# First layer of a two-layer kernel: norm, transpose and copy of a token tile issued in front of the key products of the tile ahead of it

## The chip, the cores and the metric

The kernel runs on one core of a Trainium2 chip. The metric is device time in microseconds (us). A core has a matrix engine (TensorE, PE in the profile; its weight loads are PEld), a vector engine (VectorE, DVE), an engine for activation functions and copies (ScalarE, ACT), a general engine (GpSimd, POOL) and a queue that issues most transfers (SyncE, SP). The engines run side by side and wait for each other by semaphores; each works through its own list of instructions in the order of that list. SBUF is the memory on the core from which they work, PSUM the one that TensorE writes its results to.

## The reference

One sequence of 2048 tokens of width 512, float32, passes two layers. Each layer norms the tokens and adds an attention and a feed-forward part to them. Only the head of the first layer matters here:

```python
xn = _layernorm(x, axis=-1)
x = x + _L0_attn_ref(xn, ...) + _L0_ffn_ref(xn, ...)

# in _L0_attn_ref: linear attention, 16 heads of 32
k = _heads(hidden_states @ k_w.T + k_b, b, s)
v = _heads(hidden_states @ v_w.T + v_b, b, s)
kp = jax.nn.elu(k) + 1.0
kv = jnp.einsum('bhsd,bhse->bhde', kp, v)
z = jnp.einsum('bhsd,bhd->bhs', qp, kp.sum(axis=2))[..., None]
# in _L0_ffn_ref: 8 of 16 experts for each token
probas = jax.nn.sigmoid(x2 @ Wg.T)
_, idx = jax.lax.top_k(probas + biases, K)
```

The second layer has causal attention over a window of 1024 tokens, and a block that runs attention and an MLP on an eighth of the tokens. The change doesn't touch it.

## The kernel before, in words

**The whole.** `two_layer_kernel` has one stage after another: the head stage of the first layer (keys, the sum over keys, the experts' ranks), then queries, experts and output projection in four blocks of 512 tokens, then both parts of the second layer. The change lies in the head stage, which in the profile reaches from the start to some 144 us of 1706.2.

**The loop.** The stage goes over 16 tiles of 128 tokens (`NT = 16`, `for t in range(NT)`). One round for tile t writes down, in this order:

- at t = 0, 4 and 8: the loads of the four tiles t+4 to t+7 (`load_x`, line 70, SP queue), and their mean and variance (`stats`, lines 74, 75 on VectorE; the root at line 78 on ScalarE, its reciprocal at line 79). At t = 0 the weights of the later stages are put on the SP queue too.
- the norm: `xn = (x - mean) * rstd`, one VectorE instruction (line 276); GpSimd adds the output bias to the unnormed tile (line 280), and SP stores that sum in DRAM (`res_d`, line 70).
- `transpose4` (line 110): four 128x128 transposes of `xn` on TensorE into a PSUM tile `tr`, and one ScalarE copy (line 117) from there to `xnT`.
- the key products `pk` (line 288): four matmuls of 512 columns, from `xnT` and the key weights. In the profile each float32 matmul stands as two instructions, so a tile has 8.
- the key's feature map: VectorE adds the bias (line 290, `kk`) and cuts at zero (line 293, `ke`), ScalarE takes the exponential (line 294), VectorE joins both (line 295, `kk`), and GpSimd adds the result to a running sum (line 296, `ksum`).
- `gathered(t - 1)` (line 242): four matmuls of 512 columns, `gx += kk^T xn`, for the tile before. They read its `kk` and its `xn`.
- after t = 3, 7 and 11: `gates` for the block of four tiles (products `pgp`, line 204; a ScalarE copy `gp`, line 117; products `pg`, line 212; an exponential, line 215), then `ranked` (lines 222 to 235), 23 VectorE instructions that rank the 16 experts of each token. The last block's come after the loop.

**Buffers.** Tile `x` has 8 buffers, `xn` has 3, `kk` and `ke` have 2 each, and PSUM has 2 for `tr` (shared with `pg`) and 2 for `pk` (shared with `pgp`). A buffer is reused when its last reader is done: the fourth `xn` waits for the `gathered` of the first.

**What sets the order.** The kernel is written with a framework that builds each engine's list. It doesn't keep the source's order: an instruction that is ready by its own estimate of times may go ahead of an earlier one that isn't, and among those that are ready the one written first goes first. The trace shows both: the transposes of tiles 1 and 2 stand side by side on TensorE at 14.14 us, and one pair of `gx` instructions of the tile before stands between a tile's transposes and its `pk`. Once built, a list is fixed.

Of the kernel before, what the change touches and what calls it, by code (L numbers as in the profile page):

```python
# [12 lines left out]
F32 = mybir.dt.float32  # L13
BF16 = mybir.dt.bfloat16
AF = mybir.ActivationFunctionType
ALU = mybir.AluOpType
# [3 lines left out]
P = 128  # L20
T = 2048
NT = T // P
D = 512
# [15 lines left out]
def two_layer_kernel(ctx: ExitStack, tc: tile.TileContext, a: dict, out: bass.AP):  # L39
    nc = tc.nc  # L40
    V, S, G, PE = nc.vector, nc.scalar, nc.gpsimd, nc.tensor
# [4 lines left out]
    def const(shape, name, pool=cpool, dtype=F32):  # L46
        return pool.tile(shape, dtype, tag=name, name=name)
# [19 lines left out]
    res_d = tc.dram_tile([T, D], F32, name="res_d")  # L67

    def load(eng, dst, src):
        eng.dma_start(out=dst, in_=src)  # L70
# [35 lines left out]
    def transpose4(pool, src_of, dst, name, copy, tag="tr"):  # L106

        tp = pool.tile([P, NC, P], F32, tag=tag, name=name)
        for c in range(NC):
            PE.transpose(tp[:, c, :], src_of(c), ident)  # L110
        copy(dst, tp)
# [16 lines left out]
    with ExitStack() as l0:  # L128
# [3 lines left out]
        def weight(name, shape, src, pool=w0):  # L132
            t = const(shape, name, pool)
            load(nc.sync, t, src)
            return t

        xnT = [const([P, NC, TB], f"xnT{b}", xp) for b in range(NTB)]
# [6 lines left out]
        with ExitStack() as p1:  # L144
            w1 = p1.enter_context(tc.tile_pool(name="w1", bufs=1))
            wk1 = p1.enter_context(tc.tile_pool(name="wk1", bufs=2))
            ps_kv = p1.enter_context(tc.tile_pool(name="ps_kv", bufs=1, space=PSUM))
            ps1 = p1.enter_context(tc.tile_pool(name="ps1", bufs=2, space=PSUM))

            kc = "(c p) o -> p c o"  # L150
            x = {}

            def load_x(t):
                x[t] = wk1.tile([P, D], F32, tag="x", name=f"x_{t}", bufs=8)
                load(nc.sync, x[t], a["x"][t * P : (t + 1) * P, :])
# [15 lines left out]
            ob = weight("ob", [P, D], a["o_b"].partition_broadcast(P), w1)  # L171
# [17 lines left out]
            mv = const([P, NT, 2], "mv", w1)  # L189
            rstd = const([P, NT], "rstd", w1)  # L190
            def stats(lo, hi):
                for t in range(lo, hi):
                    layernorm_stats(wk1, mv[:, t, :], x[t], f"st_{t}")
                rsqrt_into(rstd[:, lo:hi], mv[:, lo:hi, 1], eps5)
# [4 lines left out]
            def gates(b):  # L199


                parts = ps1.tile([P, TB], F32, tag="mm", name=f"pgp_{b}")
                for c in range(NC):
                    PE.matmul(
                        parts[c * HD : (c + 1) * HD, :], WgT[:, c, :], xnT[b][:, c, :],
                        start=True, stop=True, skip_group_check=True,
                    )
                gp = wk1.tile([P, TB], F32, tag="gp", name=f"gp_{b}", bufs=1)
                scopy(gp, parts)
                pg = ps1.tile([P, 4, E], F32, tag="tr", name=f"pg_{b}")  # L210
                for i in range(4):
                    PE.matmul(
                        pg[:, i, :], gp[:, i * P : (i + 1) * P], fold, start=True, stop=True
                    )
                S.activation(prob[:, 4 * b : 4 * b + 4, :], pg, AF.Exp, scale=-1.0)

            def ranked(b):

                pr = prob[:, 4 * b : 4 * b + 4, :]
                V.tensor_scalar_add(pr, pr, 1.0)
                V.reciprocal(pr, pr)
                sc = wk1.tile([P, 4, E], F32, tag="sc", name=f"sc_{b}", bufs=1)
                V.tensor_tensor(sc, pr, rb.unsqueeze(1).to_broadcast([P, 4, E]), ALU.add)
                for i in range(4):
                    other = sc[:, i, :].unsqueeze(1).to_broadcast([P, E, E])
                    own = sc[:, i, :].unsqueeze(2).to_broadcast([P, E, E])
                    gt = wk1.tile([P, E, E], F32, tag="gt", name=f"gt_{b}_{i}")
                    eq = wk1.tile([P, E, E], F32, tag="eq", name=f"eq_{b}_{i}")  # L230
                    V.tensor_tensor(gt, other, own, ALU.is_gt)
                    V.tensor_tensor(eq, other, own, ALU.is_equal)
                    V.tensor_tensor(eq, eq, tie, ALU.mult)
                    V.tensor_tensor(gt, gt, eq, ALU.add)
                    V.tensor_reduce(rank[:, 4 * b + i, :], gt, AX.X, ALU.add)
# [4 lines left out]
            def gathered(t, kk, xn):  # L240
                for g in range(NC):
                    PE.matmul(  # L242
                        gx[g], kk[:, g * P : (g + 1) * P], xn, start=t == 0, stop=t == NT - 1
                    )

            before = None
            for t in range(NT):
                tok = slice(t * P, (t + 1) * P)
                xt = xnT[t // 4][:, :, t % 4 * P : (t % 4 + 1) * P]
                if t % 4 == 0 and t + 4 < NT:  # L250
                    for u in range(t + 4, t + 8):
                        load_x(u)
                    stats(t + 4, t + 8)
                if t == 0:
                    q_b = weight("q_b", [P, NC], a["q_b"])

                    q_wT = weight("q_wT", [P, NC, D], a["q_wT"].rearrange(kc, p=P))
                    WdT = weight("WdT", [P, NC, LAT], a["WdT"].rearrange(kc, p=P))
                    sw1T = weight("sw1T", [P, NC, HID], a["sw1T"].rearrange(kc, p=P))
                    swgT = weight("swgT", [P, NC, HID], a["swgT"].rearrange(kc, p=P))  # L260
                    rw1T = weight("rw1T", [P, E, HID], a["rw1T"])
                    rwgT = weight("rwgT", [P, E, HID], a["rwgT"])
                    rw2T = weight(
                        "rw2T", [P, 2, E, LAT], a["rw2T"].rearrange("(b p) e l -> p b e l", p=P)
                    )
                    o_wT = weight("o_wT", [P, NC, D], a["o_wT"].rearrange(kc, p=P))
                    sw2T = weight("sw2T", [P, 2, D], a["sw2T"].rearrange(kc, p=P))
                    WuT = weight("WuT", [P, D], a["WuT"])
                    wr = weight("wr", [P, D], a["w_router"].partition_broadcast(P))
                    for j in range(2):  # L270
                        load(
                            nc.sync, w_qk[:, :, j * D : (j + 1) * D],
                            a["w_qkv"][:, j * D : (j + 1) * D].rearrange(kc, p=P),
                        )
                xn = wk1.tile([P, D], F32, tag="xn", name=f"xn_{t}", bufs=3)
                V.tensor_scalar(
                    xn, x[t], mv[:, t, 0:1], rstd[:, t : t + 1], ALU.subtract, ALU.mult
                )

                G.tensor_tensor(x[t], x[t], ob, ALU.add)  # L280
                load(nc.sync, res_d[tok, :], x[t])
                transpose4(
                    ps1, lambda c: xn[:, c * P : (c + 1) * P], xt, f"tr_{t}", scopy
                )

                pk = ps1.tile([P, D], F32, tag="mm", name=f"pk_{t}")
                for c in range(NC):
                    PE.matmul(pk, xt[:, c, :], k_wT[:, c, :], start=c == 0, stop=c == NC - 1)  # L288
                kk = wk1.tile([P, D], F32, tag="kk", name=f"kk_{t}")
                V.tensor_tensor(kk, pk, kb, ALU.add)  # L290

                ke = wk1.tile([P, D], F32, tag="ke", name=f"ke_{t}")
                V.tensor_scalar_min(ke, kk, 0.0)
                S.activation(ke, ke, AF.Exp)
                V.scalar_tensor_tensor(kk, kk, 0.0, ke, ALU.max, ALU.add)
                G.tensor_tensor(ksum, ksum, kk, ALU.add)
                if before is not None:
                    gathered(*before)
                before = t, kk, xn
                if t % 4 == 3 and t < NT - 1:  # L300
                    gates(t // 4)
                    ranked(t // 4)
# [34 lines left out]
        with ExitStack() as p3:  # L337
# [127 lines left out]
            for b in range(NTB):  # L465
# [76 lines left out]
                for i in range(TB // P):  # L542
                    t = b * (TB // P) + i
                    xr.append(wk.tile([P, D], F32, tag="xr", name=f"xr_{t}", bufs=4))
                    load(nc.sync, xr[i], res_d[t * P : (t + 1) * P, :])
                for i in range(TB // P):
                    t = b * (TB // P) + i
                    tok = slice(i * P, (i + 1) * P)
# [448 lines left out]
    with ExitStack() as p5:  # L997
# [226 lines left out]
        for ch in range(NFC):  # L1224
            wd = stream(a["w_down"][ch * D : (ch + 1) * D, :], f"wd_{ch}")
            for i in range(NC):
                f = ch * NC + i
# [203 lines left out]
    for Q, g in order:  # L1431
# [3 lines left out]
        for n, unit in enumerate(group.us):  # L1435
            name = f"{Q}_{g}_{n}"
# [71 lines left out]
```

## Time and profile before

| What | Value |
|---|---|
| Median of 3 runs | 1710.7 us (1710.59 to 1712.12) |
| Profiled execution, its own time | 1707.93 us |
| Its span, first to last instruction | 1706.2 us |
| Head stage, from the first transpose to the first one of the gathered `gx` | 5.7 to 143.7 us |
| TensorE busy in that stage | 132.75 of 138.0 us |
| VectorE, ScalarE, GpSimd busy in that stage | 79.02, 33.62, 41.72 us |
| `tr` transposes, `pk` and `gx` instructions in the trace | 64, 128, 128 |
| One `xn` on VectorE (line 276): shortest, median, longest | 539, 546, 1362 ns |
| One `kk` join on VectorE (line 295): shortest, median, longest | 678, 693, 1789 ns |
| One copy `xnT` on ScalarE (line 117), median | 586 ns |

A row of the timeline has a start, a duration, an engine, a line, the operation, what it writes and reads, and how many instructions are merged in it; in square brackets is the idle time of the engine ahead of it, and what ended it. The end of a matmul is modelled, so the time from start to start says more than a duration. Stretches are given in us from the start of the span.

### The profile page before, as it was taken

What the parts mean: (1) busy time and instruction counts of PE and PEld (TensorE: products, weight loads), DVE (VectorE), ACT (ScalarE), POOL (GpSimd) and SP (SyncE); (2) the same over time, 40 slices, a digit from 0 to 9 for tenths busy, and PEclk for the clock granted to TensorE, in tenths of its full rate; (3) what the DMA queues carried; (4) which work ended last, traced back from release to release, by engine and by line L of the source; (5) the groups of instructions that cost most, each with busy time, mean ns of one, the idle gap of its engine ahead of it and who ended that gap; (6) DMA issues with size and microseconds to landing.
All of it is one profiled execution on the core that took longest, in us unless ns stands there. A gap on an engine that the chain in (4) does not pass through costs nothing.

```text
span 1706.2 us, 20420 instructions
## 1 busy us (share of the span) xinstructions
PE 1658.3 (97%) x8114; PEld 744.2 (44%) x8114; DVE 972.9 (57%) x1240; ACT 596.2 (35%) x955; POOL 499.6 (29%) x398
## 2 busy tenths in 40 slices
PE   8999999999999999999999989999999999999999
PEld 3445444444444444444443434454564333433343
DVE  4755646344445544356566676775554477556565
ACT  3213333243253344222121220440100576447473
POOL 3230000000000200053565425230000677558584
PEclk9999999999999999999999999999899999999999
DMA  9411001120030431121011034112222300110101
GB/s 362 168 38 47 25 25 37 46 90 25 25 111 25 94 105 50 51 68 56 25 27 31 28 105 167 62 50 75 74 99 75 100 1 2 50 51 2 50 2 38
DMA packets 62384, 109.22 MB, mean 64 GB/s; under 512 B 12529, under 2 KB 14065, under 8 KB 61521
## 3 DMA queue, kind: packets, MB, share of 16 engines
q1 hardware_dynamic: 55856, 106.12, 18.4%
q0 software_dynamic: 1152, 1.21, 0.4%
q10 hardware_dynamic: 5280, 0.59, 0.4%
q8 instruction: 63, 1.03, 0.2%
q14 instruction: 33, 0.26, 0.1%
HBM read 86.24 MB, written 21.67 MB: 63 GB/s over the span
## 4 chain that ended last, share of the span: by engine, by line
PE 83%; DVE 10%; ACT 2%; issue 2%; POOL 1%; DMA 1%; SPq 0%; DVEq 0%; POOLq 0%; ACTq 0%
PE eg L492 6%; PE ea L494 6%; PE acc L478 6%; PE pa L633 6%; PE ps L1300 6%; PE p L965 6%; PE av L1374 6%; PE po L553 3%; PE pq L367 3%; PE po L1344 3%; PE gx L242 3%; DVE mx L645 3%; PE pk L288 2%; PE mg L1214 2%; PE pm L1229 2%; PE sg L403 2%
## 5 line engine op out<-in xcount | busy, mean ns | idle before, releaser
L645 DVE TENSOR_REDUCE mx<-pa 128x4 f32<-128x1536 f32 (+3 forms) x144 | 252.8, 1756 | 160.5 <-PE pa L641 77.6
L1407 POOL TENSOR_TENSOR acc<-acc,pt 128x1024 f32<-128x1024 f32 (+2 forms) x110 | 252.7, 2325 | 96.7 <-DVE acc L1407 43.4
L1334 ACT ACTIVATE pt<-ps 128x1024 f32<-128x1024 f32 (+3 forms) x208 | 181.4, 924 | 108.1 <-PE ps L1323 61.5
L1407 DVE TENSOR_TENSOR acc<-acc,pt 128x1024 f32<-128x1024 f32 (+1 forms) x80 | 144.4, 1833 | 103.8 <-POOL acc L1407 103.8
L633 PE MATMUL pa<-kT,qT 32*128 32x384 f32 (+3 forms) x1152 | 139.8, 539 | 17.9 <-DVE mx L645 17.4
L350 ACT ACTIVATE r_e<-eg 128x512 f32<-128x512 f32 x128 | 75.8, 594 | 202.2 <-PE eg L492 195.7
L1300 PE MATMUL ps<-qT,kT 32*128 32x512 f32 (+3 forms) x1152 | 139.9, 525 | 0.0
L352 DVE TENSOR_TENSOR h<-ea,r_e 128x512 f32<-128x512 f32 x128 | 87.1, 684 | 85.1 <-ACT r_e L351 84.1
L743 POOL TENSOR_TENSOR cosg<-cosg,gam 128x512 f32<-128x512 f32 x2 | 2.5, 1264 | 442.6 <-DVE gam L740 442.6
L492 PE MATMUL eg<-xl,rwgT 128*128 128x512 f32 x256 | 130.8, 592 | 0.0
L494 PE MATMUL ea<-xw,rw1T 128*128 128x512 f32 x256 | 130.7, 592 | 0.0
L478 PE MATMUL acc<-h,rw2T 128*128 128x512 f32 x256 | 129.3, 592 | 0.0
L965 PE MATMUL p<-w_qk,xnt 128*128 128x512 f32 x256 | 124.2, 608 | 2.0 <-DVE qk L758 1.9
L1374 PE MATMUL av<-pt,v 128*32 128x512 f32 (+3 forms) x1024 | 100.8, 482 | 0.0
L1300 PEld LDWEIGHTS ps<-qT,kT 32*128 32x128 f32 x1152 | 54.7, 183 | 94.6 <-issue 65.7
L633 PEld LDWEIGHTS pa<-kT,qT 32*128 32x128 f32 x1152 | 46.6, 184 | 101.8 <-DVE mx L645 69.2
L488 DVE TENSOR_TENSOR xw<-xw,xl 128x512 f32<-128x512 f32 x64 | 43.8, 685 | 82.4 <-DMA xw<-w_d 82.2
L351 ACT ACTIVATE r_e<-r_e 128x512 f32<-128x512 f32 x128 | 80.3, 629 | 5.5 <-ACT r_e L350 1.8
L478 PEld LDWEIGHTS acc<-h,rw2T 128*128 128x128 f32 x256 | 48.7, 190 | 61.2 <-issue 53.7
L494 PEld LDWEIGHTS ea<-xw,rw1T 128*128 128x128 f32 x256 | 48.7, 190 | 61.2 <-issue 59.3
L492 PEld LDWEIGHTS eg<-xl,rwgT 128*128 128x128 f32 x256 | 48.7, 190 | 61.2 <-issue 60.7
L288 PE MATMUL pk<-k_wT,xnT 128*128 128x512 f32 x128 | 62.1, 629 | 3.6 <-ACT xnT L117 3.6
(336 smaller groups left out, 2419.7 us busy)
## 6 DMA issues: line engine op xcount, KB each, us to landing
xw<-w_d SPq DMA_DIRECT2D x64, 256.0 KB, 3.2
x<-in_x SPq DMA_DIRECT2D x16, 256.0 KB, 4.0
res_d<-x SPq DMA_DIRECT2D x16, 256.0 KB, 2.7
xr<-res_d SPq DMA_DIRECT2D x16, 256.0 KB, 4.1
xn_d<-xn SPq DMA_DIRECT2D x16, 256.0 KB, 2.9
res_d<-xr SPq DMA_DIRECT2D x16, 256.0 KB, 3.1
xnq<-xn_d SPq DMA_DIRECT2D x16, 256.0 KB, 2.7
v_d<-vt SPq DMA_DIRECT2D x16, 256.0 KB, 2.0
```

What stands on the lines that cost most here:

```text
L288: PE.matmul(pk, xt[:, c, :], k_wT[:, c, :], start=c == 0, stop=c == NC - 1)
L352: V.tensor_tensor(dst, pa, r, ALU.mult)
L478: PE.matmul(acc, rw2T[:, j, e, :], h, start=e == 0 and j == 0, stop=e == E - 1 and j == 1,)
L492: PE.matmul(pg, rwgT[:, e, hb], xl, start=True, stop=True)
L494: PE.matmul(pa, rw1T[:, e, hb], xw, start=True, stop=True)
L633: PE.matmul(pS[:, h, : w * P], qT[r, g, i * P : (i + 1) * P], kT[r, g, ks], start=True, stop=not (edge or last),)
L645: V.tensor_reduce(mx[:, g, :, c], pS[:, :, : w * P], AX.X, ALU.max)
L965: PE.matmul(pj, xnt[:, c, :], w, start=c == 0, stop=c == NC - 1)
L1300: PE.matmul(pS[h // 2][:, h % 2, t0 * P - q0 : (t1 + 1) * P - q0], kT[r, g, kb * P : (kb + 1) * P], qT[r, g, t0 * P : (t1 + 1) * P], start ...
L1334: S.activation(pT[:, :, :n], pS[hp][:, :, :n], AF.Exp)
L1374: PE.matmul(self.av[h * HD : (h + 1) * HD, t0 * P - o : (t1 + 1) * P - o], vs[kb // 4][:, kb % 4, hs], got[h // 2][:, h % 2, t0 * P - q0 : ...
L1407: eng.tensor_tensor(part, part, got[hp][:, :, : q1 - q0], ALU.add)
```

## The change

The norm, the GpSimd add, its store, the transposes and the copy become a function `transposed(t)`, and each round calls it for tile t+1 ahead of the key products of tile t. Tile 0's is called in its own round, so round 0 writes down those of tiles 0 and 1 before the first `pk`. The instructions are the same ones in the same number; no buffer is added.

```diff
+            def transposed(t):
+                xn = wk1.tile([P, D], F32, tag="xn", name=f"xn_{t}", bufs=3)
+                V.tensor_scalar(
+                    xn, x[t], mv[:, t, 0:1], rstd[:, t : t + 1], ALU.subtract, ALU.mult
+                )
+
+                G.tensor_tensor(x[t], x[t], ob, ALU.add)
+                load(nc.sync, res_d[t * P : (t + 1) * P, :], x[t])
+                transpose4(
+                    ps1, lambda c: xn[:, c * P : (c + 1) * P],
+                    xnT[t // 4][:, :, t % 4 * P : (t % 4 + 1) * P], f"tr_{t}", scopy,
+                )
+                return xn
+
             before = None
             for t in range(NT):
-                tok = slice(t * P, (t + 1) * P)
                 xt = xnT[t // 4][:, :, t % 4 * P : (t % 4 + 1) * P]
...
-                xn = wk1.tile([P, D], F32, tag="xn", name=f"xn_{t}", bufs=3)
-                V.tensor_scalar(
-                    xn, x[t], mv[:, t, 0:1], rstd[:, t : t + 1], ALU.subtract, ALU.mult
-                )
-
-                G.tensor_tensor(x[t], x[t], ob, ALU.add)
-                load(nc.sync, res_d[tok, :], x[t])
-                transpose4(
-                    ps1, lambda c: xn[:, c * P : (c + 1) * P], xt, f"tr_{t}", scopy
-                )
-
+                xn = xn_next if t > 0 else transposed(0)
+
+                if t + 1 < NT:
+                    xn_next = transposed(t + 1)
                 pk = ps1.tile([P, D], F32, tag="mm", name=f"pk_{t}")
                 for c in range(NC):
                     PE.matmul(pk, xt[:, c, :], k_wT[:, c, :], start=c == 0, stop=c == NC - 1)
```

## The prediction

> **What bounds the kernel now.** I read the page first. TensorE is busy 97% of the span, and the chain that ended last runs through it:
>
> ```profile
> PE 1658.3 (97%) x8114; PEld 744.2 (44%) x8114; DVE 972.9 (57%) x1240; ACT 596.2 (35%) x955; POOL 499.6 (29%) x398
> ...
> PE 83%; DVE 10%; ACT 2%; issue 2%; POOL 1%; DMA 1%; SPq 0%; DVEq 0%; POOLq 0%; ACTq 0%
> ```
>
> So only idle TensorE time in the head stage can be won. The table of stretches shows where that is; its columns are the stretch, its length, then busy us (instructions) of PE, PEld, DVE, ACT, POOL:
>
> ```profile
> 14.20:36.70 22.50, 22.26 (x61) 10.04 (x59) 12.40 (x23) 8.33 (x11) 10.65 (x8) 1.00 1.04 402
> 36.70:51.10 14.40, 13.67 (x49) 6.25 (x48) 11.41 (x29) 2.61 (x5) 3.93 (x3) 1.00 1.04 389
> 51.10:69.50 18.40, 18.39 (x48) 8.15 (x48) 10.49 (x20) 5.16 (x7) 5.56 (x5) 1.00 0.56 182
> 69.50:86.80 17.30, 15.24 (x56) 7.36 (x56) 14.94 (x40) 7.11 (x12) 5.59 (x5) 1.00 0.12 46
> ```
>
> Stretches without ranking (14.2, 51.1) have next to no idle TensorE time. Those with ranking (36.7, 69.5, and 103.6 with 13.64 of 14.40) lose 0.7 to 2.1 us each, and there VectorE is busy 11.4 to 14.9 us. The whole stage has 138.0 - 132.75 = 5.25 us.
>
> Then TensorE's timeline: a plain tile, and the end of the first ranking.
>
> ```profile
> 29.25 0.60 PE L110 MATMUL tr<-ident,xn 128*128 128x128 f32 x4
> 29.69 1.02 PE L242 MATMUL gx<-xn,kk 128*128 128x512 f32 x2
> 30.55 3.68 PE L288 MATMUL pk<-k_wT,xnT 128*128 128x512 f32 x8
> ...
> 46.06 0.60 PE L110 MATMUL tr<-ident,xn 128*128 128x128 f32 x4
> 47.34 3.70 PE L288 MATMUL pk<-k_wT,xnT 128*128 128x512 f32 x8 [0.68 <-ACT xnT L117]
> ```
>
> In the plain tile a pair of `gx` instructions of the tile before fills the time of the copy: from transposes to `pk` 1.30 us, 0.86 of them work. At 46.06 no `gx` is ready, and `pk` waits for the copy: 47.34 - 46.06 = 1.28, where transposes alone take 29.69 - 29.25 = 0.44. The loss is 0.84 us. What holds `gx` back there is on VectorE:
>
> ```profile
> 47.97 0.41 DVE L235 TENSOR_REDUCE rank<-gt 128x16 f32<-128x256 f32 x1
> 48.30 0.42 DVE L293 TENSOR_SCALAR ke<-kk 128x512 f32<-128x512 f32 x1
> 48.63 0.54 DVE L276 TENSOR_SCALAR xn<-x,mv,rstd 128x512 f32<-128x512 f32 x1
> 49.47 1.59 DVE L295 SCALAR_TENSOR_TENSOR kk<-kk,ke 128x512 f32<-128x512 f32 x1 [0.30 <-ACT ke L294]
> ```
>
> The `kk` of tile 4 is complete at 51.06, and `gx` starts at 51.11, just as `pk` ends (51.04). Two chains end together here.
>
> **The change part by part.** I count against the profiled execution, 1707.93 us (span 1706.2 and 1.7 around it). It lies 2.8 below the median of the runs shown, 1710.7; I add differences to the median.
>
> *What is removed: waits for the copy.* With the transposes of t+1 ahead, `pk(t)` is always ready behind them. Waits of 0.84 stand at 46.06, 79.63, 84.44 and 112.93: 4 x 0.84 = 3.4. At 71.29 `pg` waits for the copy `gp` (1.77 from start to start, against 39.50 - 38.69 = 0.8 for the work of `pg`, and 1.0 for that of `pgp`): 0.8, which `pk` of the next tile now fills. At 14.14 to 15.41, two tiles' transposes and a wait take 1.27 against 0.88: 0.4. Together 4.6 us.
>
> *Where these stalls go.* All but the last lie in the ranking stretches. Take the first. The transposes of tile 4 now precede `gates`, so `pgp` starts 0.44 later; a pair of `pk` (0.86) in front of `pg` stands where a pair of `gx` stood, with some 0.3 of shift. The chain `pg`, exponential, 23 ranking instructions, `kk` keeps its length, so `gx` of tile 4 starts about 0.75 later than 51.11. TensorE no longer waits for the copy but for `kk`. In that time it does more: the transposes of tile 6 (0.44; their `xn` is there at 49.2) and one pair of `pk` of tile 6 (0.86). Net 1.3 - 0.75: 0.5 won. PSUM's two `pk` buffers allow no more. The third ranking looks the same (`gx` at 117.99, `kk` join of 1.59 at 116.34). In the second, `gx` at 86.84 hangs on a ScalarE chain with two table loads (80.87 and 83.23, 1.28 each), and I take 0.5 there too. Three times 0.5, and 0.4 at the start: 1.9 us stay of 4.6. The bounds are 0 (all goes into waiting for `kk`) and 4.6.
>
> *What is added: `xn` on a short leash.* `xn(t+1)` reuses the buffer of `xn(t-2)`, whose last reader is `gathered(t-2)`, now the work just before `transposed(t+1)` on TensorE. Before, that wait had most of a tile to spare. Now TensorE can put one pair of `pk(t)`, 0.86 us, in between. This is VectorE and GpSimd at such a point:
>
> ```profile
> 28.84 1.27 POOL L296 TENSOR_TENSOR ksum<-ksum,kk 128x512 f32<-128x512 f32 x1 [1.90 <-DVE kk L295]
> ```
>
> ```profile
> 29.45 0.94 DVE L276 TENSOR_SCALAR xn<-x,mv,rstd 128x512 f32<-128x512 f32 x1 [0.76 <-PE gx L242]
> ```
>
> `gx` ends at 29.41, `xn` starts at 29.45 and takes 0.94 instead of the median 0.546: it ends at 30.39, 0.28 after the GpSimd add that overlaps it (30.11). The same 0.28 follows the adds at 54.35 and 95.70. The Trainium skill, "SBUF — State Buffer", section "SBUF: two separate sides", has a rule for it that speaks against this change: VectorE and GpSimd share a port pair under an exclusive lock, and the later one blocks until the other is done. This trace agrees in effect, apart from the 0.28. Free of the lock: 0.04 + 0.55, and 0.15 from the end of `xn` to the first transpose (5.63 to 5.78), 0.74; that hides under 0.86 and costs nothing. With it: 0.04 + 0.94 + 0.15 = 1.13, so TensorE stands 0.27. The `ksum` add falls at this point in each plain tile (it starts some 3.0 us after `pk` ends, and `gx` takes 3.44), so I take the locked value for the 8 tiles outside the rankings: 8 x 0.27 = 2.2 us. Bounds: 0, if the list has two pairs ahead of the transposes; 5.6, if each `xn` took the longest one's 1.36 (0.69 each).
>
> *What is moved at the start.* `transposed(1)` is written before `pk(0)`. `pk(0)` starts at 7.54; its instructions take 0.85 each instead of 0.43, although the granted clock reads 1.00. `xn(1)` needs the statistics of tiles 1 to 3 (one root for all three), and its data arrive in turn: on VectorE it starts at 12.36 and is done at 12.9. The list is fixed before the run. If it has the transposes after `pk(0)`, nothing changes; before its last pair (12.66), TensorE waits 0.4; before the third (10.96), 2.1; before the whole, 5.4. VectorE's list, with `xn` of tiles 1 and 2 just before the `kk` of tile 0, suggests that its builder expects them late in `pk(0)`. I take 1.0, with 0 and 5.4 as the ends. A gain is excluded: the data arrive as before.
>
> *The other moved instructions* come at nothing. The GpSimd add (1.27 us) goes ahead of `ksum`, which is read only after 144 us. The store `res_d` moves up with it on SP: that of tile 4 is now ahead of the loads of tiles 8 to 11. SP blocks there anyway for a free `x` buffer; the loads go out at 51.45 and their statistics start at 62.25. If that cover were gone, tile 8's transposes would come after `pk(7)`, as before.
>
> Sum: -1.9 + 2.2 + 1.0 = +1.3 us. In the profile 1707.9 would become 1709.2, and the median 1710.7 becomes 1712.0.
>
> **The rivals.** *The gain stays.* The list has two pairs of `pk` ahead of the transposes, the first tile's stay behind `pk(0)`, and the extra transposes cover the wait for `kk`. Then the whole 4.6 goes: 1706.1. For it: each of these waits names the copy. Against: at 51.06 and 51.11 VectorE ends with TensorE, so a shorter wait there is given back.
>
> *The first tile waits, and it is slower.* The builder takes the arrival of tiles 1 to 3 to be early and puts all four transposes ahead of `pk(0)`. Nothing can refill the loss, since every later product follows. The price is 5.4, and -1.9 + 2.2 of the rest: 1710.7 + 5.7 = 1716.4. It decides over 0.2% from a wait of about 3 us, that is from a place ahead of `pk(0)`'s second pair. For it: `ident`'s reduction, written before all statistics, stands after the statistics of tile 1 on VectorE, so the builder's times at the start aren't the chip's. Against: `xn(1)` stands late on VectorE's list.
>
> *It does nothing:* the builder already reorders (tile 2's transposes are ahead of `pk(1)`), and fillers merely change names: 1710.7.
>
> **How the numbers follow.** The small sum has a chance of 0.48, with its own range of 1709 to 1714; no effect 0.12; the gain that stays 0.12; the first tile's wait 0.28. A measurement of this kernel can tell 0.2%, 3.4 us, from no change: faster is below 1707.3, slower above 1714.1. Faster 0.12, within 0.60, slower 0.28. The range goes from 1706.8, just above the full gain, to 1716.6, just past the first tile's wait.
>
> **What would show it.** TensorE's timeline should have no wait for `xnT` outside the first tile, and idle time ended by `kk` (line 295) at the first `gx` after each ranking. If `xn` costs what I think, transposes carry waits for `xn` of 0.2 to 0.5 us in plain tiles. The first tile shows in the start of the second tile's `pk`: 15.4 before, over 18 if the rival holds. I'm wrong if the ranking stretches shorten by over 1 us each, or if a stretch after 144 us changes its length: I assume that the later lists stay as they are.

## The result, and the profile after

The changed kernel takes 1715.45 us (8 runs, 1713.31 to 1717.18), beside 1710.77 for the kernel before in the same comparison: 1.0030 of it, 95% interval 1.002 to 1.004. A later comparison gave 1713.24 beside 1707.81, 1.0035 (1.0022 to 1.0049). It is slower by 4.7 to 5.4 us, 0.3%.

The profiled execution took 1715.81 us, its span is 1714.0, 7.8 more than before. TensorE's busy time has risen by 2.0 us only:

```profile
PE 1660.3 (97%) x8114; PEld 744.7 (43%) x8114; DVE 973.9 (57%) x1240; ACT 596.0 (35%) x955; POOL 499.2 (29%) x398
```

The first transpose of the gathered sums, which ends the head stage, starts at 150.96 instead of 143.67: 7.3 of the 7.8 us are there. Behind it every engine's list has the same order as before. The stretches of the stage again (length, then busy us of PE, PEld, DVE, ACT, POOL, then TensorE's granted clock); the first line is the kernel before, the others are the changed one:

```profile
5.70:14.20 8.50, 7.75 (x13) 3.45 (x14) 3.95 (x10) 0.88 (x2) 0.00 (x0) 1.00 0.95 329
...
5.70:14.20 8.50, 4.89 (x9) 1.92 (x9) 3.58 (x10) 0.89 (x2) 0.00 (x0) 1.00 1.03 332
14.20:36.70 22.50, 22.18 (x59) 10.09 (x60) 10.85 (x21) 8.38 (x11) 10.40 (x8) 0.92 1.03 398
...
86.80:103.60 16.80, 13.82 (x32) 6.19 (x32) 7.71 (x12) 4.13 (x6) 5.07 (x4) 0.80 0.08 32
```

TensorE stands in two places: ahead of 14.2 us, where 4.89 us of work are left of 7.75, and behind 86.8 us, where a clock of 0.80 comes on top. (By then the stage runs some 4 us late, so a stretch with the same bounds no longer holds the same work; the table of intervals below compares like with like.) TensorE's timeline shows the first place, before and after:

```profile
7.54 6.76 PE L288 MATMUL pk<-k_wT,xnT 128*128 128x512 f32 x8 [0.68 <-ACT xnT L117]
14.14 1.04 PE L110 MATMUL tr<-ident,xn 128*128 128x128 f32 x8
15.41 4.56 PE L288 MATMUL pk<-k_wT,xnT 128*128 128x512 f32 x10 [0.24 <-ACT xnT L117]
...
7.51 3.78 PE L294 MATMUL pk<-k_wT,xnT 128*128 128x512 f32 x4 [0.68 <-ACT xnT L117]
14.18 0.70 PE L110 MATMUL tr<-ident,xn 128*128 128x128 f32 x4 [2.88 <-DVE xn L248]
14.67 3.58 PE L294 MATMUL pk<-k_wT,xnT 128*128 128x512 f32 x4
18.08 0.60 PE L110 MATMUL tr<-ident,xn 128*128 128x128 f32 x4
18.52 4.46 PE L294 MATMUL pk<-k_wT,xnT 128*128 128x512 f32 x10
```

The list has tile 1's transposes in the middle of tile 0's key products, and they wait 2.88 us for `xn`. The second tile's `pk` starts at 18.52 instead of 15.41. (Line 248 is the norm, 294 `pk`, 296 to 301 `kk` and `ke`; in the kernels of some experiments these numbers are one or two higher.) The second place is the second ranking, again before and after:

```profile
71.29 1.06 PE L212 MATMUL pg<-fold,gp 128*128 128x16 f32 x8 [0.71 <-ACT gp L117]
...
80.90 3.70 PE L288 MATMUL pk<-k_wT,xnT 128*128 128x512 f32 x8 [0.68 <-ACT xnT L117]
84.44 0.60 PE L110 MATMUL tr<-ident,xn 128*128 128x128 f32 x4
85.71 1.13 PE L288 MATMUL pk<-k_wT,xnT 128*128 128x512 f32 x2 [0.67 <-ACT xnT L117]
...
83.32 3.60 PE L294 MATMUL pk<-k_wT,xnT 128*128 128x512 f32 x8
88.54 0.66 PE L110 MATMUL tr<-ident,xn 128*128 128x128 f32 x4 [1.62 <-DVE xn L248]
90.55 2.08 PE L294 MATMUL pk<-k_wT,xnT 128*128 128x512 f32 x2 [1.36 <-ACT xnT L117]
```

Tile 10's transposes wait 1.62 for `xn`, and its `pk` then 1.36 for the copy, which the change was to hide; the pair of `pk` takes 1.87 from start to start instead of 0.86. The old list stood here too, 0.71, 0.68 and 0.67 us, 2.1 in all; the new one stands 3.0. Here is VectorE at that time in the changed kernel:

```profile
86.29 0.41 DVE L234 TENSOR_TENSOR gt<-gt,eq 128x256 f32<-128x256 f32 x1
...
87.29 0.40 DVE L235 TENSOR_REDUCE rank<-gt 128x16 f32<-128x256 f32 x1
87.62 0.41 DVE L299 TENSOR_SCALAR ke<-kk 128x512 f32<-128x512 f32 x1
87.95 0.54 DVE L248 TENSOR_SCALAR xn<-x,mv,rstd 128x512 f32<-128x512 f32 x1
```

Tile 10's `xn` needs the buffer of tile 7, whose last reader is the `gx` pair that runs from 82.47 to 83.3. By then the ranking has had VectorE for 4 us (from 79.19), and `xn` comes out behind it. ScalarE has a part in both waits. The ranking begins 5.6 us behind the start of the gates (73.58), where it took 3.1 before (72.65 - 69.52): `pg` stands behind two pairs of `gx` and a tile's transposes, and the exponential behind a table load of 1.28 us (77.64). And the copy that `pk` waits for starts only at 89.93, 0.7 us behind the last transpose, since ScalarE is in another table load (88.10) and the exponential of a `ke`.

For comparing kernels I cut the stage where the first `pgp` of each block starts (the first three gates) and at its end. All numbers are from TensorE's timelines.

| Kernel (label) | start to 1st gates | 1st to 2nd | 2nd to 3rd | 3rd to end | stage ends |
|---|---|---|---|---|---|
| before | 36.73 | 32.79 | 34.08 | 40.07 | 143.67 |
| before, second profile (before_again) | 37.08 | 32.79 | 34.08 | 40.06 | 144.01 |
| after | 40.90 | 32.68 | 38.57 | 38.81 | 150.96 |
| after, second profile (after_again) | 40.58 | 32.68 | 35.60 | 38.80 | 147.66 |
| tile1_late | 38.31 | 32.69 | 37.29 | 38.80 | 147.09 |
| only_tile1 | 40.45 | 32.78 | 34.03 | 40.06 | 147.32 |
| xn4 | 40.46 | 32.19 | 32.49 | 38.30 | 143.44 |
| both | 38.26 | 32.18 | 33.24 | 38.29 | 141.97 |
| before_xn4 | 36.93 | 32.27 | 32.70 | 39.54 | 141.44 |
| before_ranks_late | 36.78 | 32.42 | 33.44 | 39.89 | 142.53 |
| after_ranks_late | 40.67 | 33.11 | 33.40 | 39.22 | 146.40 |
| after_split | 38.37 | 32.68 | 35.59 | 38.80 | 145.44 |
| xn4_split | 39.07 | 32.18 | 32.50 | 38.31 | 142.06 |

An interval of the same lists repeats to 0.03 us, except where the start or the clock enters. Under the new order one tile's transposes (0.44) lie ahead of the first and the third gates that lay behind them before.

### The profile page after: what moved, and what is told of

It reads as the page before. It is cut to its first block, busy times and chain, and to the rows that moved or that the text cites. A ratio compares the mean times of both kernels' runs of the same rounds, so it can differ in the third digit from the quotient of the medians.

```text
span 1714.0 us, 20422 instructions
## 1 busy us (share of the span) xinstructions
PE 1660.3 (97%) x8114; PEld 744.7 (43%) x8114; DVE 973.9 (57%) x1240; ACT 596.0 (35%) x955; POOL 499.2 (29%) x398
## 3 DMA queue, kind: packets, MB, share of 16 engines
q8 instruction: 63, 1.03, 0.3%
## 4 chain that ended last, share of the span: by engine, by line
PE 82%; DVE 10%; ACT 2%; POOL 2%; issue 2%; DMA 1%; SPq 0%; DVEq 0%; POOLq 0%; ACTq 0%
PE ea L500 6%; PE eg L498 6%; PE acc L484 6%; PE ps L1306 6%; PE pa L639 6%; PE p L971 6%; PE av L1380 5%; PE po L559 3%; PE pq L373 3%; PE po L1350 3%; PE gx L242 3%; DVE mx L651 3%; PE pk L294 2%; PE mg L1220 2%; PE pao L1182 2%
```

## The experiments

Theory A: the loss is the wait for tile 1, and a longer second ranking. Theory B: it is the `xn` buffers, on which norm and transposes now hang too closely. The expectations count from 1710.8 us for the kernel before; in the later comparisons it took 1707.6 to 1707.8, so the differences count, not the absolute times.

**Tile 1 behind tile 0's key products (tile1_late).**

```diff
-                if t + 1 < NT:
+                if 0 < t < NT - 1:
                     xn_next = transposed(t + 1)
...
+                if t == 0:
+                    xn_next = transposed(1)
```

> The change, but in round 0 tile 1 is normed, transposed and copied behind the key products of tile 0 instead of ahead of their second half. Theory A (the loss is a wait for tile 1 inside the first key products, 3.1 us in the trace, plus a longer second ranking stretch): the second tile's key products start at about 15.4 us as before the change, and the time falls by about 3.1 us from 1715.4 to 1712.3. Theory B (the loss comes from the xn buffers: norm and transposes now follow the gathered products of three tiles ahead too closely): no more than 0.5 us is won, 1715. Both expect the second ranking stretch to stay long.

Measured: 1709.47 beside 1707.59, 1.0013 (1.0006 to 1.0021). From start to first gates 38.31, 2.3 to 2.6 less than the changed kernel.

```profile
14.10 1.17 PE L110 MATMUL tr<-ident,xn 128*128 128x128 f32 x8
15.44 4.56 PE L294 MATMUL pk<-k_wT,xnT 128*128 128x512 f32 x10 [0.16 <-ACT xnT L117]
20.54 3.70 PE L242 MATMUL gx<-xn,kk 128*128 128x512 f32 x8 [0.54 <-DVE kk L303]
```

The second tile's key products start at 15.44, as before; then the first `gx` waits 0.54 for its `kk`, which takes part of the gain. The second ranking stays long. Against the changed kernel's +4.7 to +5.4, +1.9 is left: about the 3.1 us that theory A expected are won.

**Tile 1 alone (only_tile1).** The kernel before, with one tile moved:

```diff
-                xn = xn_next if t > 0 else transposed(0)
-
-                if t + 1 < NT:
-                    xn_next = transposed(t + 1)
+                xn = xn_next if t == 1 else transposed(t)
+
+                if t == 0:
+                    xn_next = transposed(1)
```

> The kernel before, with tile 1 alone moved ahead of the key products of tile 0; all other tiles in their own rounds. Theory A: the wait for tile 1 is there in full and nothing refills it, 1710.8 + 3.1 = 1713.9, with the ranking stretches as long as before the change. Theory B: as the kernel before, 1710.8, within 0.5.

Measured: 1710.44 beside 1707.59, 1.0016 (1.0005 to 1.0026), +2.9. The stage is 3.3 to 3.7 us longer than before, all of it ahead of the first gates; the other three intervals are those of the kernel before to 0.05. That is more than the wait of 2.44, since in this profile the clock was full only from 19.44 us on, and two of the second tile's `pk` instructions ran at half rate as well.

```profile
7.38 3.78 PE L294 MATMUL pk<-k_wT,xnT 128*128 128x512 f32 x4 [0.68 <-ACT xnT L117]
13.60 1.11 PE L110 MATMUL tr<-ident,xn 128*128 128x128 f32 x4 [2.44 <-DVE xn L248]
14.51 7.77 PE L294 MATMUL pk<-k_wT,xnT 128*128 128x512 f32 x12
```

So the first tile is a cost of its own, as theory A has it, and most of the change's.

**Four buffers for xn (xn4).**

```diff
-                xn = wk1.tile([P, D], F32, tag="xn", name=f"xn_{t}", bufs=3)
+                xn = wk1.tile([P, D], F32, tag="xn", name=f"xn_{t}", bufs=4)
...
-                gs.append(wk1.tile([P, D], F32, tag="gs", name=f"gs_{g}", bufs=4))
+                gs.append(wk1.tile([P, D], F32, tag="x", name=f"gs_{g}", bufs=8))
```

> The change with four buffers for xn instead of three (the space comes from the gathered sums, which take the tile buffers of x at the end of the loop). Theory A: only the small waits of transposes for xn in plain tiles go, 0.17 to 0.28 us each, 0.9 in all: 1714.5; the wait of 2.9 us in the first tile stays. Theory B: most of the 4.7 us goes, 1711 to 1712, and the second ranking stretch is as short as before the change.

Measured: 1705.06 beside 1707.59, 0.9987 (0.9980 to 0.9994). The wait for tile 1 is still there (2.33 us), but the second ranking takes 32.49 instead of 35.60 to 38.57.

```profile
82.39 0.60 PE L110 MATMUL tr<-ident,xn 128*128 128x128 f32 x4
82.82 3.60 PE L294 MATMUL pk<-k_wT,xnT 128*128 128x512 f32 x8
86.93 2.81 PE L294 MATMUL pk<-k_wT,xnT 128*128 128x512 f32 x6 [0.51 <-DVE kk L296]
```

Tile 10 is transposed ahead of tile 9's key products and copied while they run (83.02); the waits of 1.62 and 1.36 are gone, and so are those in plain tiles, and 0.51 for a free `pk` buffer stands in their place. Theory A had 0.9 us for this; that was far too little. For the second ranking theory B is right, but it too expected a time no better than that of the kernel before, and this is 2.5 below it. The stage accounts for little of that: it ends 0.2 to 0.6 us earlier than in the two profiles of the kernel before. The rest lies behind the stage, where the lists are the same, and its cause is open.

**Both (both).** 

> The change with tile 1 behind the key products of tile 0 and with four buffers for xn. Theory A: 1715.4 - 3.1 - 0.9 = 1711.4, still 0.6 over the kernel before, since the second ranking stretch stays longer. Theory B: like xn4 alone, 1711 to 1712. If the second ranking stretch also heals, the time falls below the kernel before, to some 1708 to 1709.

Measured: 1704.72 beside 1707.59, 0.9986 (0.9978 to 0.9994). The stage ends at 141.97. This is the last case of the expectation, 2 to 3 us below the kernel before, and looks like a success of the new order. The next run is its control.

**The old order with four buffers (before_xn4).** The second diff of xn4, on the kernel before.

> Control: the kernel before (source order unchanged) with four buffers for xn and the gathered sums in the buffers of x. If the 2.5 to 2.9 us that the two runs with four buffers and the new order are below the kernel before come from the order, this stays at the kernel before within 0.5 us, and its first ranking still shows a wait of 0.68 us for the copy. If they come from the buffers alone, it is 2 to 3 us below it as well.

Measured: 1705.9 beside 1707.81, 0.9991 (0.9981 to 1.0). The stage ends at 141.44, ahead of every kernel with the new order. The wait of 0.68 that was expected if the order made the gain isn't there:

```profile
46.26 1.04 PE L110 MATMUL tr<-ident,xn 128*128 128x128 f32 x8
47.53 3.70 PE L288 MATMUL pk<-k_wT,xnT 128*128 128x512 f32 x8 [0.24 <-ACT xnT L117]
```

With a fourth buffer the list builder puts two tiles' transposes side by side, and the wait for the copy falls from 0.68 to 0.24 without any change of the source's order. What beats the kernel before is the buffer: 2.2 us of stage, 1.9 of the median. (The two edits were not run apart; the gathered sums come up only at the end of the loop, so what is won ahead of the third gates, 1.7 us, is put down to `xn`.) On the medians the kernels with four buffers (1704.72 to 1706.11) can't be told apart: their intervals overlap.

**The changed kernel once more (after_again).** 

> The changed kernel as it is, once more, beside the kernel before on one chip. The four runs so far put the wait for tile 1 at 2.4 to 2.9 us and the second ranking, from one gates to the next, 4.5 us longer than before, of which about 2 are matrix work at half rate. If that is the rule and no accident of one profile, the trace shows the waits for xn (1.6) and for xnT (1.4) again, pairs of pk and gx behind them at 1.0 to 1.4 us instead of 0.86, and the time is 4 to 7 us above the kernel before. If it was an accident, the second ranking takes 34 us as before the change.

Measured: 1713.24 beside 1707.81, 1.0035 (1.0022 to 1.0049). The waits of 2.96, 1.62 and 1.36 are there again, to the hundredth in the ranking. The half rate behind them isn't:

```profile
88.22 0.65 PE L110 MATMUL tr<-ident,xn 128*128 128x128 f32 x4 [1.62 <-DVE xn L248]
90.23 1.12 PE L294 MATMUL pk<-k_wT,xnT 128*128 128x512 f32 x2 [1.36 <-ACT xnT L117]
91.20 3.60 PE L242 MATMUL gx<-xn,kk 128*128 128x512 f32 x8
```

`pk` and `gx` run at full rate, and the interval is 35.60: the 38.57 of the first profile held 2.97 us that half rate cost. Without it the stage ends at 147.66, 3.7 to 4.0 behind the kernel before.

**The rankings behind the loop (before_ranks_late, after_ranks_late).** In both, `ranked` of the first three blocks is written behind the loop.

```diff
-                    ranked(t // 4)
...
-            ranked(NTB - 1)
+            for b in range(NTB):
+                ranked(b)
```

> The kernel before with the rankings of the first three blocks moved behind the loop (same instructions, other place; gates stay). It prices the rankings inside the loop. No wait of TensorE for kk or for a copy should be left in the loop, which ends some 3 us earlier; behind it the 69 ranking instructions of 0.34 us, about 24 us, lie open on VectorE in part.

> The changed kernel with the same move. Without rankings in the loop VectorE norms a tile as soon as its buffer is free. If the rankings are what makes the buffer of xn dear, the loop here is longer than that of the kernel before with the same move only by the wait for tile 1 (2.4 to 2.9 us, and 0.4 to 0.8 more while the clock is low) and by the small waits for xn in plain tiles (0.2 to 0.3 us each, 1 to 2 in all): 4 us, with the matrix work at its full rate. If the buffer costs as much without rankings, it is 7 us or more.

Measured: 1706.28 (0.9992, 0.9982 to 1.0002) and 1708.79 (1.0008, 0.9996 to 1.002), both beside 1707.81. The edit didn't do what I meant: the builder filled free VectorE time with the rankings, inside the loop as before, only behind everything else that was ready. So these runs don't price the absence of a ranking, and the expected 3 us of a shorter loop can't be read from them. They show that with rankings of low rank the stage is 3.87 us longer under the new order (146.40 and 142.53), 3.9 of it ahead of the first gates, and that `xn` is then late by single ranking instructions: tile 6's transposes wait 1.19. The second ranking isn't longer under the new order here (33.40 and 33.44).

```profile
50.18 1.44 DVE L232 TENSOR_TENSOR eq<-sc 128x256 f32<-128x256 f32 x1
51.54 0.53 DVE L248 TENSOR_SCALAR xn<-x,mv,rstd 128x512 f32<-128x512 f32 x1
```

**Tile 1's statistics on their own (after_split, xn4_split).**

```diff
-            stats(1, 4)
+            stats(1, 2)
+            stats(2, 4)
```

> The changed kernel, with the statistics of tile 1 closed on their own (one more root and reciprocal, of tile 1 alone) instead of with those of tiles 2 and 3. Its list has the transposes of tile 1 ahead of the whole first key products, but tile 1 lands at about 7.3 us, so they can run at about 9.5 instead of 13.6 to 14.2. If the loss at the start is the wait for the data of tiles 2 and 3, the first key products begin at about 10.5 and the first gates at about 39, some 1.5 us earlier than 40.6 in the changed kernel, and the time falls by 1.5. If the wait is for something else, the first gates stay at 40.6.

> The same with four buffers for xn. If the start and the buffers add up, the head stage ends 1.5 us ahead of the run with four buffers alone (143.4), at about 142, still no shorter than the kernel before with four buffers (141.4): the new order itself wins nothing once its two costs are gone.

Measured: after_split 1709.66 beside 1707.58, 1.0014 (1.0007 to 1.0022); xn4_split 1706.11, 0.9990 (0.9982 to 0.9999).

```profile
9.74 1.12 PE L110 MATMUL tr<-ident,xn 128*128 128x128 f32 x4 [2.90 <-DVE xn L249]
10.65 5.48 PE L295 MATMUL pk<-k_wT,xnT 128*128 128x512 f32 x8
```

Tile 1's transposes come 4 us earlier, and the first gates at 38.37 instead of 40.58 to 40.90: 2.2 us won, more than the 1.5 I expected. What TensorE waited for was the data and statistics of tiles 2 and 3. In xn4_split tile 1's own data came later (its statistics start at 9.43 instead of 7.67), and the stage ends at 142.06, again not ahead of before_xn4, as was expected.

**The kernel before once more (before_again).** 

> The kernel before once more, for a second look at its head stage: if its first profile is typical, the stage ends at 143.7 us within 0.5, and the second ranking, from one gates to the next, takes 34.1 us with all matrix work at its full rate.

Measured: 1707.41 in one execution; the stage ends at 144.01, and the second ranking takes 34.08. The first profile was typical.

## Why the prediction was right and wrong

The measured +4.7 to +5.4 us lies in the stated range, but beyond the small sum's own range (up to 1714): the likeliest case, +1.3 and no change that can be told, didn't come about. The slower rival, with a chance of 0.28, did, and its sign too: the second tile's `pk` starts at 18.52. That its total of 5.7 comes so near is in part luck. It rested on transposes ahead of all of `pk(0)`, 5.4, while the list has them in its middle; later data, half rate and the second ranking made up the difference. Of the other signs, `kk` ends the idle time at the first `gx` behind the first and the third ranking, but a wait for `xnT` is left at 90.55. Two terms of the sum failed, the start and the leash, and the third held in part:

- **Start: mis-sized.** The step took 1.0 us. The list has the transposes ahead of the third pair, for which the prediction had 2.1, and tile 1's `xn` starts at 13.57 instead of 12.36, since tile 3 landed later; in the second profile of the kernel before it starts at 13.01, so the landing differs from one execution to the next. Waits measured 2.3 to 3.0 in five profiles with this place in the list. `only_tile1` shows the term alone: 3.3 to 3.7 us of stage. The list's place was open and the price was known for each place; "late in `pk(0)`" was read from VectorE's list, which said when `xn` is ready, not where TensorE's list would have it.
- **The short leash: right mechanism, wrong place.** In plain tiles I had 8 waits of 0.27. There are four, of 0.17, 0.28, 0.16 and 0.27, 0.9 us; in each `xn` takes 0.92 to 1.04 us and ends 0.28 behind a GpSimd add, as forecast. In the other tiles `xn` hardly meets an add, or TensorE has more work in front. The price was in the second ranking, where the sum had booked a gain of 0.5: there `xn` not only waits for `gx` but then stands behind the ranking, 1.62 us, and the copy behind it 1.36, and at times TensorE then runs at half rate. Set against the old waits of 2.1, the loss there is 1.1 us without half rate. `xn4` takes all of this away.
- **Stalls that move: right for the first and third ranking.** The waits for the copy at the first and third ranking are gone, and this stands in their place:

```profile
53.58 0.60 PE L110 MATMUL tr<-ident,xn 128*128 128x128 f32 x4
55.29 3.70 PE L242 MATMUL gx<-xn,kk 128*128 128x512 f32 x8 [1.10 <-DVE kk L301]
```

  From the first gates to this `gx` it takes 55.29 - 40.90 = 14.39 us, and took 51.11 - 36.73 = 14.38 before: VectorE's chain sets it. Of the 0.84 nothing is won but the transposes of one tile, done meanwhile.
- **The rest of the balance.** Against before, `after_again` has +3.85, -0.11, +1.52 and -1.27 in the four intervals, 4.0 in all. With the 0.44 of transposes that change sides put back, that is +3.4 for the start, +0.3, +1.1 for the second ranking, and -0.8 behind the third gates. No run takes this last gain apart; the timelines show that the last block's `pgp`, which the old list split around the last `gx` with 1.0 us for two of its eight instructions, is now in one piece of 1.0. With four buffers the new order has this gain too (38.29 to 38.31 against 39.54), but loses 0.9 to 3.1 us at the start, the 0.44 taken off.
- **Stage and median.** The stage says +4.0 without half rate in the second ranking and +7.3 with it, and the medians lie between. That half rate comes in some executions and not in others was seen in profiles; how often it comes was not counted.
- **Moved add and store: as said.** No wait for them is on TensorE's path.
- **Two bounds** are off by 0.1: 8 x 0.69 is 5.5, and the wait ahead of all of `pk(0)`, with the same 0.15 as the others, is 5.5. Nothing rests on them.

## What to carry to other kernels

Ask of every step that is moved forward what its buffer waits for, and what has meanwhile taken the engine on which it must then run: a wait of no length on a free engine is a long one behind 23 queued instructions. At the start of a loop a step moved ahead meets data that haven't landed. And before an order is credited with a gain, run the old order with the same extra buffer: here the stage with four buffers ends at 141.44 in the old order and at 141.97 or later in the new.

## What the runs showed of the hardware

**Half rate comes in whole windows.** In the 13 profiles each stretch with a granted clock of 0.5 lasts 3.41 us or a multiple of it, except the last of a profile, which the end cuts off. In `after` the first three such stretches start at 14.65, 89.75 and 792.89 us, 22 and 206 windows of 3.413 us apart. So the bounds between windows are known where no drop is, too. Four profiles have the same pair of waits in the second ranking (1.61 to 1.62 and 1.36 us, with a tile's transposes between; 3.6 us from the last `pk` to the next). Cut at the bounds, `after` has

```profile
86.34:89.75 3.41, 1.24 (x6) 0.42 (x4) 3.38 (x9) 1.64 (x2) 1.19 (x1) 1.00 0.00 0
89.75:93.17 3.42, 2.62 (x3) 1.18 (x4) 2.65 (x3) 1.28 (x3) 1.67 (x3) 0.50 0.20 77
93.17:96.58 3.41, 3.41 (x5) 1.35 (x4) 0.00 (x0) 0.00 (x0) 0.95 (x1) 0.50 0.01 2
```

and `after_again`, with the same waits,

```profile
85.45:88.86 3.41, 1.79 (x7) 0.61 (x5) 3.38 (x10) 1.08 (x1) 0.62 (x1) 1.00 0.00 0
88.86:92.27 3.41, 2.04 (x6) 1.06 (x6) 3.10 (x3) 1.84 (x4) 1.91 (x2) 1.00 0.20 77
```

In `after` and `tile1_late` most of the gap lies in one window, TensorE is busy in it for 1.24 and 1.03 us (0.58 and 0.37 without the transposes), and the next window is at half rate. In `after_again` and `after_split` a bound splits the gap, both windows hold 1.79 to 2.05 us, and the clock stays. The Trainium skill, "TensorE: Matmul & The Clock Gate", Part 1, has the clock halved after an idle window of about 3.4 us that runs free of the kernel. Length and free run agree with this; the window need not have been idle here. Part 4 says that a transpose doesn't count as busy in the same way; no run here can tell, since the two groups stay apart with the transposes and without them. In the kernel before, with waits of at most 0.71 between 14 us and the stage's end, no drop was seen in the stage in two profiles.

**At the start** the trace's first record of the clock is the full one, at 13.73 us in `before`, 11.24 in `after`, 19.44 in `only_tile1`. Ahead of it the column reads 1.00 for want of a record, while `pk` instructions take 0.85 us instead of 0.43. In `after` the full clock came while TensorE stood and was gone again from 14.65 to 18.06, the 0.92 of the table: the second half of `pk(0)` ran at half rate.

**Half rate behind the stage.** Each of the 13 profiles has three to six such windows there, not always at the same places, and each can cost up to 1.7 us (an estimate: half its length); `before` has six of them, `xn4` four. The 64 executions of the kernel before on one chip lay between 1703.0 and 1710.9 us, and the span follows the granted clock (median 1701.7 at 0.998, 1708.4 at 0.993). A difference of 1 us in the head stage is read off the trace's intervals, which repeat to 0.03, and not off such a median.
